# Two lists, pairs of tiles and single tiles, for both mixture-of-experts layers of a decoder kernel

## The chip, the cores and the metric

The kernel runs on one core of a Trainium2 chip. A core has five engines with queues of their own: TensorE (PE, matrix products), VectorE (DVE), ScalarE (ACT), GpSimd (POOL) and SyncE (SP, which here only issues DMAs). They meet through semaphores. The metric is the device time of one execution in microseconds (us), lower is better; where several executions were timed, their median is given.

## The reference

A decoder of two layers works on `x`, four batches of 512 tokens with 256 features (2048 tokens). Each layer is a cross-attention to a context and a feed-forward network (FFN), each behind a layer norm and with a residual sum. What matters here are the two FFNs, both with routed experts, all in float32:

```
FFN0: 8 experts, top 2 of each token, hidden width 1024
  cap = ceil(ceil(2048*2*1.25)/8) = 640 rows per expert, later rows are dropped
  h = silu(buf @ Wg.T) * (buf @ Wu.T)      W12 = [Wg; Wu], 2048 x 256 per expert
  y = h @ W3.T                             summed back with the routing weights
FFN1: 15 experts, top 3 of each token, hidden width 256, no cap
  a = gelu(g) * xh * mult ; y = a @ fc2.T  weighted sum over the 3 experts
  plus a shared expert of width 512 for every token
```

Which rows an expert gets is only known on the chip, from the router's logits. With the given inputs the kept rows per expert are 484, 320, 640, 193, 463, 226, 595, 640 in FFN0 and 678, 325, 314, 88, 187, 462, 437, 202, 452, 364, 887, 345, 474, 458, 471 in FFN1.

## The kernel before, in words

**Stages.** Attention 0 goes through the four batches; behind each batch, `route` normalises its tokens, finds the experts and ranks, and scatters the rows with indirect DMAs (the "puts", L381, on POOL) into a buffer in HBM where each expert has a region of its own (`slots` for FFN0, `xs` for FFN1). Then comes the loop over FFN0's tiles, attention 1 with the routing of FFN1, and the loop over FFN1's tiles. A tile is 128 rows of one expert, a pair is 256 neighbouring rows of one expert.

**Lists.** `listing` (L405) counts the rows of every expert and works out, in some 18 small DVE operations over all experts at once, a list of (expert, row block) entries. Two selector matmuls (L461) bring it into one row, from which SP later loads registers: `fetch0`/`fetch1` load an entry's rows with a register address, then its expert's weights. `listing` is a generator: at each `yield` it hands the turn back.

**FFN0.** After two batches a first list names three (`AHEAD`) full pairs; these are computed in the tail of attention 0 (`some_pairs`), under the routing of the last batch. In that last batch, the second list is made inside `route`, in `counted`, that is ahead of the ranks and the puts. It holds single tiles: what the three pairs have not taken. `ALWAYS0` = 24 of them always run, more of them stand in nested `If`s. For a single tile, `hidden0` puts two blocks of 128 columns into one PSUM tile (L1006, 64 matmul instructions of 128 columns), `output0` multiplies with W3 (L1024, 16 instructions of 256 columns). Every entry loads 3 MB of weights (L153) into a ring of three places; the loads stand on SP behind the entry's rows (L969).

**FFN1.** Every expert's first pair is in the program without a list, so its weights and rows have fixed addresses; the list holds further pairs, 15 of which always run. `hidden` (L1307) and the output (L1361) work with 256 rows. Weights (L1160/L1161, or L1163/L1164 with a register) have a ring of three, rows (L1332) a ring of five. The list is made after the puts of the last batch, in the tail of attention 1, where PE works through the shared expert's pieces (L1188, L1203) with their gate on DVE (L1174, L1177). Results are scattered by indirect DMAs on POOL (L1030, L1368), and read back in order at the end (L1411).

**What sets the order.** On PE, DVE, ACT and SP the order is written out: `attention` steps through time slots; in each slot it emits its own matmuls, then lets the generators that are "going" (`route`, `listing`) advance by up to two yields, with at most one piece of PE work, and then emits one piece of the other work (an AHEAD pair's piece, or a shared expert's). The first thing that PE, DVE or SP meets in its queue therefore blocks what stands behind it. The loops run as `pipeline`: in iteration p it fetches entry p+2, turns (transposes) p+1, computes the hidden part of p and the output of p-1. The last entries' `values_load` brings the length of the list into registers of all engines, for the `If`s.

## Time and profile before

Three runs took 1203.73, 1205.29 and 1206.92 us (median 1205.29).

| | |
|---|---|
| profiled execution, its own time | 1215.69 us |
| its span, first to last instruction | 1214.0 us |
| mean granted TensorE clock | 0.955 |
| PE busy | 1149.4 us (95%), 6582 instructions |
| DVE busy | 620.4 us (51%) |
| ACT busy | 459.5 us (38%) |
| POOL busy | 186.5 us (15%) |
| moved by DMA | 204.73 MB, mean 169 GB/s |
| loads of W12 and W3 | 27 each (2048 and 1024 KB) |
| loads of rows for FFN0 | 3 of 258 KB, 24 of 129 KB |
| loads of rows, w1 and fc2 for FFN1 | 30 each (258, 515 and 256 KB) |

By stages, PE busy: 270.92 us of 0 to 300 (attention 0), all of 320 to 540 (FFN0), 278.53 us of 600 to 880 (attention 1), all of 1050 to 1160 (FFN1), 27.74 us of the last 54.

A matmul in float32 shows as two instructions. Matmuls are pipelined and their ends are modelled, so a row's duration holds a tail that the next one overlaps: a pitch is read from start to start. "[1.05 <-DMA rows<-slots]" behind a line means that its engine sat idle for 1.05 us before it, until that transfer had landed.

### The profile page before, as it was taken

The page shows a single profiled execution, that of the slowest core. Times are in us where ns is not written, and L with a number is a line of the kernel's source. Part 1 is how long each engine was busy: PE and PEld are TensorE (multiplying, and loading weights), DVE is VectorE, ACT ScalarE, POOL GpSimd, SP SyncE. Part 2 cuts the span into 40 slices and gives each one's busy share as a digit, 9 for nine tenths or more (in the row PEclk, how much of TensorE's full clock was granted, in tenths as well). Part 3 has the DMA queues.
Part 4 walks back from the last instruction along what each step waited for, and adds up shares of the span by engine and source line. Part 5 has one row for each costly group of instructions (what it writes and reads, how often), then busy time and mean ns, then how long its engine had stood idle before and what let it go on. Part 6 is the DMA issues. An engine that isn't in the chain of part 4 may idle for free.

```text
span 1214.0 us, 18265 instructions
## 1 busy us (share of the span) xinstructions
PE 1149.4 (95%) x6582; PEld 738.3 (61%) x6582; DVE 620.4 (51%) x1591; ACT 459.5 (38%) x877; POOL 186.5 (15%) x274
## 2 busy tenths in 40 slices
PE   6999997999999999999999999999999999999982
PEld 3334432788999999997433333433336558888862
DVE  6677773531111111114768688867636435444426
ACT  3365464421222222223266576575653102333320
POOL 2000112042000000002000000211322402333330
PEclk7899998999999999999699999999989989999996
DMA  8999107227788888863101000001100135777737
GB/s 321 406 403 403 69 27 264 75 92 292 302 306 326 316 312 305 317 253 106 35 1 36 1 1 1 27 27 36 44 25 28 53 114 160 218 236 214 226 122 244
DMA packets 64405, 204.73 MB, mean 169 GB/s; under 512 B 9502, under 2 KB 31922, under 8 KB 57392
## 3 DMA queue, kind: packets, MB, share of 16 engines
q1 hardware_dynamic: 56144, 182.93, 42.3%
q0 software_dynamic: 8160, 20.52, 4.6%
q8 instruction: 55, 0.90, 0.3%
q14 instruction: 46, 0.38, 0.1%
HBM read 138.57 MB, written 66.70 MB: 169 GB/s over the span
## 4 chain that ended last, share of the span: by engine, by line
PE 44%; DMA 5%; DVE 4%; issue 1%; ACT 0%; POOL 0%; SPq 0%; DVEq 0%; POOLq 0%
PE sc L696 10%; PE av L735 5%; PE shared L1188 4%; PE pg L1307 3%; PE pv L1307 3%; PE pyp L1361 3%; PE sct L720 3%; DMA y<-ysb,rows 2%; DMA yr<-y 2%; PE pp L673 2%; DVE negmax L701 2%; PE shared L1203 1%; PE po L792 1%; PE pa L645 1%; PE pa L673 1%
## 5 line engine op out<-in xcount | busy, mean ns | idle before, releaser
L701 DVE TENSOR_REDUCE negmax<-sc 128x1 f32<-128x512 f32 x384 | 245.6, 683 | 67.8 <-PE sct L720 59.2
L725 ACT ACTIVATE es<-sct 128x512 f32<-128x512 f32 x384 | 208.5, 596 | 155.2 <-PE sct L720 143.6
L696 PE MATMUL sc<-kT,qT 32*128 32x512 f32 x768 | 255.5, 680 | 5.2 <-DVE negmax L701 2.8
L720 PE MATMUL sct<-qa,kT 32*128 32x512 f32 x768 | 254.3, 660 | 1.7 <-DVE qa L711 1.7
L696 PEld LDWEIGHTS sc<-kT,qT 32*128 32x128 f32 x768 | 82.6, 194 | 103.8 <-DVE negmax L701 59.8
L1015 DVE TENSOR_TENSOR hT<-pu,sg 128x256 f32<-128x256 f32 x96 | 40.8, 425 | 136.5 <-PE pu L1006 131.6
L735 PE MATMUL av<-es,v 128*32 128x512 f32 x768 | 107.2, 619 | 0.1
L1006 PE MATMUL pg<-rT,w 128*128 128x128 f32 x768 | 101.5, 275 | 0.1
L1006 PE MATMUL pu<-rT,w 128*128 128x128 f32 x768 | 101.4, 275 | 0.0
L720 PEld LDWEIGHTS sct<-qa,kT 32*128 32x128 f32 x768 | 78.9, 188 | 26.6 <-issue 16.7
L1006 PEld LDWEIGHTS pg<-rT,w 128*128 128x128 f32 x768 | 93.5, 192 | 0.4 <-issue 0.3
L1006 PEld LDWEIGHTS pu<-rT,w 128*128 128x128 f32 x768 | 93.5, 192 | 0.0
L1024 PE MATMUL py<-w,hT 128*128 128x256 f32 x384 | 86.7, 379 | 0.0
L1368 POOL DMA_INDIRECT y<-ysb,rows x60 | 59.0, 984 | 155.1 <-ACT ysb L1366 143.5
L1024 PEld LDWEIGHTS py<-w,hT 128*128 128x128 f32 x384 | 71.2, 190 | 8.7
L1011 ACT ACTIVATE sg<-pg 128x256 f32<-128x256 f32 x96 | 36.8, 383 | 101.5 <-PE pg L1006 100.5
L378 POOL COPY rows<-weight 128x2 f32<-128x2 f32 (+1 forms) x28 | 4.2, 205 | 434.5 <-DVE weight L341 258.6
L735 PEld LDWEIGHTS av<-es,v 128*32 128x32 f32 x768 | 16.0, 109 | 76.7 <-issue 70.6
L1307 PE MATMUL pg<-rTp,wp 128*128 128x256 f32 x240 | 61.8, 380 | 0.6 <-DVE rTp L1345 0.6
L1307 PE MATMUL pv<-rTp,wp 128*128 128x256 f32 x240 | 61.6, 379 | 0.0
L1030 POOL DMA_INDIRECT y<-ysb,rows x24 | 23.6, 982 | 238.7 <-ACT ysb L1028 236.3
L1174 DVE TENSOR_SCALAR aTp<-pv,wp 128x256 f32<-128x256 f32 x60 | 32.6, 544 | 51.4 <-PE pv L1307 48.3
(257 smaller groups left out, 1490.3 us busy)
## 6 DMA issues: line engine op xcount, KB each, us to landing
w<-in_W12T_dram SPq DMA_DIRECT2D x27, 2048.0 KB
xs<-empty SPq DMA_DIRECT2D x61, 516.0 KB
w<-in_W3T_dram SPq DMA_DIRECT2D x27, 1024.0 KB
wp<-in_w1p_dram SPq DMA_DIRECT2D x30, 515.0 KB
yr<-y SPq DMA_DIRECT2D x20, 512.0 KB
rows<-xs SPq DMA_DIRECT2D x30, 258.0 KB
wp<-in_fc2T_dram SPq DMA_DIRECT2D x30, 256.0 KB
slots<-empty SPq DMA_DIRECT2D x11, 516.0 KB
```

The costliest lines, as they stand in the source:

```text
L696: nc.tensor.matmul(sc, q[u][32 * j : 32 * j + 32, qt * P : (qt + 1) * P], k[u][32 * j : 32 * j + 32, :], start=True, stop=True,)
L701: nc.vector.tensor_reduce(heads[:, qt, j, HELP[s] : HELP[s] + 1], sc, AX.X, ALU.max, negate=True)
L720: nc.tensor.matmul(sc, k[u][32 * j : 32 * j + 32, kt * P : (kt + 1) * P], qa[u][32 * j : 32 * j + 32, :], start=True, stop=True,)
L725: nc.scalar.activation(t, sc, AF.Exp, scale=p["scale"])
L735: nc.tensor.matmul(av[b, g][32 * j : 32 * j + 32, :], vs[b % NV][:, kt, h : h + 32], es[u, kt, j], start=(first and kt == 0), stop=(last a ...
L1006: nc.tensor.matmul(ph[:, i * n : (i + 1) * n], w[:, c, col + i * P : col + (i + 1) * P], rT[:, c, :], start=(c == 0), stop=(c == DC - 1),)
L1011: nc.scalar.activation(sg, pg, AF.Silu)
L1015: nc.vector.tensor_tensor(h, pu, sg, ALU.mult)
L1024: nc.tensor.matmul(py, hT[f][:, i * P : (i + 1) * P], w[:, f, :], start=(f == 0), stop=(f == NF - 1))
L1188: nc.tensor.matmul(ph, w1[:, c, col : col + P], ffn1.xT[b][:, c, :], start=(c == 0), stop=(c == DC - 1),)
L1307: nc.tensor.matmul(ph[:, :n], w1[:, c, col : col + P], rhs[:, c, :], start=(c == 0), stop=(c == DC - 1),)
L1368: ins = nc.gpsimd.indirect_dma_start(out=y1, out_offset=bass.IndirectOffsetOnAxis(ap=rows[:, i, D : D + 1].bitcast(I32), axis=0), in_=ysb[ ...
```

## The change

Both FFNs get two lists: pairs of tiles, and single tiles, of which an expert has at most one.

- `listing` takes a list of kinds (`steps, width, count, out`) and runs its body once for each. For pairs, an expert's number is the count of steps 128, 384, 640, ... that its rows exceed; for singles, it is the count of steps 0, 128, 256, ... less twice the pairs. The selector's counts are first copied out of PSUM. A single list takes 5 yields, two take 11.
- FFN0: after the three AHEAD pairs, 10 pairs and 4 singles always run, instead of 24 singles. `hidden0`, `turn0`, `output0` take the width of the entry from `listed0`.
- FFN1: 24 pairs and 6 singles always run, instead of 15 fixed pairs and 15 listed ones. No entry has a fixed address any more: each takes two register loads on SP, and rows and weights of the first entries are fetched one entry after another.
- `pipeline` takes the keys of the entries, pairs first; two groups of `If`s stand behind it instead of one, and two lengths are loaded.
- Pools: the turned rows and hidden tiles of FFN0 are twice as wide; the places of the weight ring go by the order of loads.

```diff
-ALWAYS0, THEN0 = 24, (25, 26, 28, MOST0)
-ALWAYS1, THEN1 = 15, (16, 17, 19, EXTRA1)
+ALWAYS0, THEN0 = (10, 4), ((11, 12, 14, E0 * (TILES0 // 2)), (5, 6, E0))
+ALWAYS1, THEN1 = (24, 6), ((25, 26, 28, (T * K1 + E1 * (P - 1)) // PAIR), (7, 8, 10, 12, E1))
...
-    def listing(f, b, pool, bank, pairs, count, steps, out, taken=None, take=0, size=1):
+    def listing(f, b, pools, bank, tiles, kinds, take=0):
...
+        counts = pools[0].tile([P, n], F32, name="list_counts", tag="list_counts")
+        nc.vector.tensor_copy(counts, number)
+        former = None
+        for pool, (steps, width, count, out) in zip(pools, kinds):
...
+            yield V
+            more = tile("more", n, steps.shape[1])
...
+            extra = tile("extra", n)
+            nc.vector.tensor_reduce(extra, more, AX.X, ALU.add)
+            front = None
+            if former is not None:
+                front = tile("front", n)
+                nc.vector.tensor_scalar(front, former, 2.0, None, ALU.mult)
+                nc.vector.tensor_tensor(extra, extra, front, ALU.subtract)
+            elif take:
+                former = tile("former", n)
+                nc.vector.tensor_copy(former, extra)
+                less, front = tile("less", n), tile("front", n)
...
+            else:
+                former = extra
+            yield V
...
+            yield V
...
+            yield V
+            nc.vector.tensor_tensor(one, named[:, :n], one, ALU.mult)
...
+            yield PEP
+            flat = bank([1, 2 * count])
+            for i in range(2):
+                nc.tensor.matmul(
+                    flat[:, i * count : (i + 1) * count], both[:, i : i + 1], ident[:, :count], start=True, stop=True
+                )
+            nc.vector.tensor_copy(out[:, : 2 * count], flat)
...
+            run(always, last=True)
+            for i, (_, more) in enumerate(then):
+                with ExitStack() as open_:
+                    for least, keys in more:
+                        open_.enter_context(tc.If(needed[i] > least))
+                        run(keys)
+
+    def keys_of(always, then, first):
+        keys = [first, first + then[0][-1]]
+        more = [
+            [(lo, list(range(k + lo, k + hi))) for lo, hi in zip((n, *t), t)] for k, n, t in zip(keys, always, then)
+        ]
+        return [k + i for k, n in zip(keys, always) for i in range(n)], more
...
+    def listed0(j):
+        if j < AHEAD:
+            return ahead0, j, AHEAD, 2
+        j -= AHEAD
+        if j < MOST0[0]:
+            return list0[0], j, MOST0[0], 2
+        return list0[1], j - MOST0[0], MOST0[1], 1
...
     def hidden0(j, new):
-        m = 1 if j < AHEAD else 2
+        m = 2 // listed0(j)[3]
         n = PAIR // m
...
             if b == B - 1:
-                yield from listing(
-                    ffn0, b, ml1, bank, TILES0, MOST0, ffn0.some, list0, ffn0.taken, AHEAD
-                )
+                kinds = list(zip(ffn0.steps, (2, 1), MOST0, list0))
+                yield from listing(ffn0, b, ml1, bank, TILES0, kinds, AHEAD)
...
             if b == B - 1:
-                yield from listing(ffn1, b, Slices(tiles1[0]()), bank, PAIRS1, EXTRA1, ffn1.some, list1)
+                yield from listing(
+                    ffn1, b, [Slices(tiles1[0]), Slices(tiles1[0])], bank, TILES1,
+                    list(zip(ffn1.steps, (2, 1), MOST1, list1)),
+                )
...
     def fetch1(p):
         if p in rows1s:
             return
         rows1s[p] = mp.tile([P, 2, ROW], F32, name="rows1", tag="rows1", bufs=5)
-        if p == 0:
-            for j in range(3):
-                w1s[j] = weights(mp, j, "wp", 3)
-        i = p - E1
-        if i < 0:
-            src = pairs1[p * PAIRS1]
-        else:
-            r = nc.sync.value_load(list1[0:1, EXTRA1 + i : EXTRA1 + i + 1], min_val=0, max_val=E1 * PAIRS1)
-            src = pairs1[bass.ds(r, 1)].rearrange("o p s d -> p (o s) d")
-        after(nc.sync.dma_start(rows1s[p], src).ins, ffn1.puts, "rows in their places")
-        e = p if i < 0 else nc.sync.value_load(list1[0:1, i : i + 1], min_val=0, max_val=E1 - 1)
-        if p not in w1s:
-            w1s[p] = weights(mp, e, "wp", 3)
+        at, i, n, m = listed1(p)
+        r = nc.sync.value_load(at[0:1, n + i : n + i + 1], min_val=0, max_val=E1 * TILES1)
+        src = tiles_1[bass.ds(r, m)].rearrange("s p d -> p s d")
+        after(nc.sync.dma_start(rows1s[p][:, :m], src).ins, ffn1.puts, "rows in their places")
+        w1s[p] = weights(mp, nc.sync.value_load(at[0:1, i : i + 1], min_val=0, max_val=E1 - 1), "wp", 3)
...
     def output1(p):
         aT, (_, w2, _), rows = aT1s.pop(p), w1s.pop(p), rows1s.pop(p)
+        m = listed1(p)[3]
...
-        for i in range(2):
+        for i in range(m):
```

`listed1` is `listed0` for FFN1, without the AHEAD branch.

## The prediction

> **What bounds the kernel now.** I read the page first (TensorE busy 1149.4 of 1214.0 us), then the table by stretches for the two FFN stages, then the timelines at their starts and ends, because an average over stages says nothing of one stage. In the stretch rows the columns are: stretch, its length, then busy us (and instructions) of PE, weight loads, DVE, ACT and POOL, granted clock, DMA share, GB/s.

> ```profile
> 320.00:540.00 220.00, 220.00 (x1665) 210.53 (x1664) 42.19 (x100) 50.11 (x122) 20.36 (x21) 1.00 0.83 313
> 1050.00:1160.00 110.00, 110.00 (x550) 96.80 (x550) 51.33 (x99) 35.01 (x79) 37.37 (x38) 1.00 0.77 226
> ```

> In FFN0 (first row) and FFN1 (second row) PE is busy without a gap, at full clock, while DMA has 17% and 23% left. So a stage gets shorter by PE time removed, not by bytes removed. The pitches, from the PE timeline:

> ```profile
> 262.38 14.06 PE L1006 MATMUL ahead<-ahead,w 128*128 128x256 f32 x64
> 276.27 13.98 PE L1024 MATMUL ahead<-w,ahead 128*128 128x256 f32 x64
> ...
> 321.91 0.38 PE L988 MATMUL prt<-ident,rows 128*128 128x128 f32 x2
> ...
> 332.74 0.38 PE L988 MATMUL prt<-ident,rows 128*128 128x128 f32 x2
> ```

> A single tile of FFN0 takes 332.74 − 321.91 = 10.83 us; a pair of FFN1 5.62 us (1148.16 to 1153.78 in the last fence, one load per pair). A pair of FFN0 exists already, under attention 0: 276.27 − 262.38 = 13.89 us for its hidden part and, for two outputs, 290.08 (the next PE line) − 276.27 = 2 × 6.90 us.

> **FFN0 loop, ten pairs.** Routing the reference's inputs gives 484, 320, 640, 193, 463, 226, 595 and 640 kept rows, 30 tiles: three pairs done ahead, then 24 singles before, ten pairs and four singles after (the constants, so no conditional part runs). A pair costs 13.89 + 6.90 + 4 transposes at 0.11 (the next instruction starts 0.43 us after four such) = 21.2 us against 2 × 10.83 = 21.65. The matmul streams 256 columns instead of twice 128, the same array time; only the weight-load-bound 0.111 us per 128 columns becomes 0.108. Gain 10 × 0.43 = **−4.3 us**. Ten expert loads of 3 MB vanish, worth nothing, since PE covers them; without that cover 30 MB at 313 GB/s would be 96 us. The four singles keep the pitch of before.

> **FFN0 start, the longer listing.** In `route` of batch 3 the listing stands ahead of the ranks and the puts. Two lists instead of one take six more yields, and the puts release the first row fetch; on SP the first expert's load waits behind that fetch:

> ```profile
> 279.09 0.97 POOL L381 DMA_INDIRECT slots<-rows,put  x1 [0.30 <-issue]
> ...
> 281.81 0.33 SPq L969 DMA_DIRECT2D rows<-slots  x1
> 283.10 0.33 SPq L153 DMA_DIRECT2D w<-in_W12T_dram  x1
> ...
> 291.52 0.44 PE L988 MATMUL prt<-ident,rows 128*128 128x128 f32 x2 [1.05 <-DMA rows<-slots]
> ```

> Today PE comes free at 290.1 and the first hidden matmul runs at 292.1: just in time, so any delay of the puts is paid. In the built order of the changed program the last pair's eight hidden pieces (1.73 us each) start at about 261.7. The second list's selector matmul stands after the second piece on PE, at 265.2, and its 17 DVE operations at some 0.2 us, behind two gate operations, end at about 267.1: PE idles 1.9 us. Put 1 then follows piece 7, and puts 2 and 3 both piece 8 (end 278.1). POOL works off 2 × 1.27 us per put, so the last scatter ends near 285.4 instead of 280.06: 5.3 us late. Two row tiles of 258 instead of 129 KB ahead add 258 KB at 421 GB/s, 0.6 us. **+5.9 us** (3.9 if the list hides and only the queue of puts stays; 6.4 with a slower DVE). Behind it stand rows, W12 and W3 of the first pairs on SP, all late together. The 1.0 us row wait that the second single had at 300 falls under a 13.9 us hidden part: **−1.0**.

> PE now idles about 6 us there. A like gap at the end of the trace:

> ```profile
> 1185.00:1190.00 5.00, 2.21 (x5) 1.85 (x6) 5.00 (x7) 0.00 (x0) 0.00 (x0) 0.50 0.62 196
> ...
> 1187.79 7.88 PE L1203 MATMUL p<-ctxT,aTs 128*128 128x256 f32 x28 [6.31 <-DVE aTs L1177]
> ```

> After 6.31 us idle the clock is 0.50 and 28 matmuls take 7.88 instead of 28 × 0.216 = 6.05 us. **+1.7** (0 to 2). The second `If` costs PE another look at a branch; the one today costs 0.64 us (FFN0) and 1.62 us (FFN1, hidden under the reads at the end): **+1.0** (0 to 2). The two register loads three entries before the end show no PE gap today: 0.

> **Attention 1's tail, the FFN1 lists.** PE carries the shared expert there, without slack:

> ```profile
> 967.88 0.26 PE L461 MATMUL bank<-ident,shared 128*1 128x23 f32 x4
> 967.99 0.81 DVE L1174 TENSOR_SCALAR shared<-shared,ctxT 128x512 f32<-128x512 f32 x1 [0.33 <-PE shared L1188]
> ```

> Today the list's last operations precede the gate (L1174) on DVE, and the selector matmul L461 finds its operand. In the changed order the gate's two operations (0.81 + 0.69 us) stand before the last five list operations (0.7 us), so L461's successor waits from 967.96 to about 970.3: 2.3 us. The second list does the same once more: seven operations (2.0 us), two gates, ten operations (1.85 us), end near 977.4 against PE's 975.7: 1.75 us. **+4.1** (1 to 5.5). [...] The trace shows granted 0.73 in 960 to 965 after 1.29 us idle behind matmuls of 16 rows. [...]

> **FFN1 loop.** Before 30 pairs (60 tiles); 54 tiles are needed (678, 325, 314, 88, 187, 462, 437, 202, 452, 364, 887, 345, 474, 458, 471 rows): after 24 pairs, six singles. A single is 16 × 0.111 + 4 × 0.216 + 2 × 0.108 = 2.86 us on PE, so 6 × (5.62 − 2.86) = **−16.5**. But its expert load stays, and SP becomes the limit:

> ```profile
> 1148.16 0.33 SPq L1164 DMA_DIRECT2D wp<-in_fc2T_dram  x1
> 1149.47 0.38 SPq L1332 DMA_DIRECT2D rows<-xs  x1
> 1150.92 0.68 SPq L1163 DMA_DIRECT2D wp<-in_w1p_dram  x1
> 1153.78 0.33 SPq L1164 DMA_DIRECT2D wp<-in_fc2T_dram  x1
> 1155.83 0.38 SPq L1332 DMA_DIRECT2D rows<-xs  x1
> ```

> L1164 waits for the end of an iteration's output; the rows of the entry three on are issued 1.31 us later (register load between) and are turned at the next iteration's end. So an iteration lasts at least 1.31 us plus the rows' landing. The rows issued at 1155.83 were used at 1158.99: landing ≤ 3.2 us for 258 KB; crowded ones took 4.3 (1025.14 to 1029.42). [...] I take the row less 129 KB at this stage's 226 GB/s: 2.7. The iterations with the first four singles would need 3.73, 2.86, 2.86, 2.86 us and get 4.0, 4.0, 4.0 and 5.5 (one list load before the end costs 2.05 − 1.31 = 0.74 us today, two 1.5): **+5.2**. [...] At the start the three weight loads no longer go out together but 3.2 us apart; they have from about 987 to 1001, so 0.

> **End.** Four scatters stand on POOL at the end today; the last is issued at 1174.82, 3 us after PE's last output, and the reads of y1 wait for it (1179.06). Two single tiles leave two: **−2.0** (−3 to 0). All else of the end is those reads.

> **Sum**: −4.3 + 5.9 − 1.0 + 1.7 + 1.0 + 4.1 + 0.5 − 16.5 + 5.2 − 2.0 = −5.4 us. Made in the profiled execution (1215.69 us, span 1214.0 and 1.7 around it), 0.9% above the median 1205.29; the terms are short, so the difference carries over: 1199.9, say **1200.0 us** (−0.44%).

> **Rivals.**
> (a) The lists hide and rows land early: list stalls 1 instead of 4.1, puts 1.9 us earlier, row stalls 0.3 instead of 5.2: −15.3, 1190. For it: DVE is half idle. Against: the built order puts gates between list operations. 12%.
> (b) Slower: the rows of the singles land late. At 4.6 us (1042.13 to 1046.75) iterations last 5.9 us, the stalls are 2.2 + 3.0 + 3.0 + 4.5 = 12.7 us, and the sum is +2.1; at 5.2 us, +4.5, 1209.8. It decides from about 4.0 us on. For it: each single still brings 771 KB of weights. Against: crowded landings come only in the first eight pairs. 17%.
> (c) No change that can be told: list prices at their upper ends (+1.4, +0.5, +1.2) give −2.3, 1203. 20%.
> (d) The loads bind FFN0: a gain of tens of us; PE's 220.00 of 220 excludes nearly all of it. 1%.
> The forecast itself, 1196 to 1203: 50%.

> **Numbers.** 0.3% (3.6 us) is what a measurement of this kernel can tell. Faster, below 1201.7: 0.43 of the 0.50, (a) and (d): 0.56. Same: the other 0.07, 0.17 of (c), and the mild part of (b), 0.04: 0.28. Slower: the rest, 0.16. Range: 1191.5 leaves out the lower part of (a), 1208.5 the upper of (b).

> **What would show it.** FFN0's first hidden matmul 6 us after AHEAD's last output, at a clock below 1; then pairs at 21.2 us. Selector matmuls waiting for DVE about 2 us three times. Last six FFN1 entries at about 4 us with waits for rows. Wrong if the first FFN0 pair starts without a gap, if singles run at 2.9 us, or if PE no longer fills the pairs.

## The result, and the profile after

The changed kernel takes 1212.1 us (median, 1208.0 to 1216.2), the kernel before on the same chip 1206.0 us (1203.6 to 1212.4): a ratio of 1.0044, 95% interval 1.0029 to 1.0058. It is slower by 5.3 us (3.5 to 7.0), where the forecast was 1200.0 us and faster. In what follows every timed run is given as its ratio to the kernel before on its own chip; 0.1% is 1.2 us.

The two profiled executions hide this. Before's took 1215.69 us, about 10 us above its median, after's 1213.86 us, about 2 above: read naively, the traces say that the change gained 1.8 us. So stages are compared here, each against as many traces as hold the same code.

First the two loops, by stretches. The columns are as in the forecast's first fence: stretch, its length, busy us (and instructions) of PE, weight loads, DVE, ACT and POOL, granted clock, DMA share, GB/s.

```profile
320.00:540.00 220.00, 220.00 (x1131) 196.19 (x1130) 40.72 (x94) 46.37 (x114) 20.62 (x21) 1.00 0.49 181
1050.00:1140.00 90.00, 90.00 (x450) 79.25 (x449) 42.07 (x81) 28.62 (x64) 31.56 (x33) 1.00 0.80 230
```

PE is still busy without a gap in both loops, at full clock. FFN0 moves 181 instead of 313 GB/s, and nothing came of that, as PE covered the loads. The loops did what was forecast. The loss lies at their ends. This is PE's timeline of the changed kernel (start, length, engine, line, tiles, and in brackets the idle time ahead and what ended it):

```profile
266.59 0.36 PE L478 MATMUL bank<-ident,list_both 128*1 128x8 f32 x4 [1.09 <-DVE list_both L471]
...
277.79 13.98 PE L1062 MATMUL ahead<-w,ahead 128*128 128x256 f32 x64
291.61 0.60 PE L1026 MATMUL prt<-ident,rows 128*128 128x128 f32 x4
299.67 1.12 PE L1026 MATMUL prt<-ident,rows 128*128 128x128 f32 x4 [7.46 <-DMA rows<-slots]
300.58 1.91 PE L1044 MATMUL pg<-rT,w 128*128 128x256 f32 x4
...
549.57 7.07 PE L1062 MATMUL py<-w,hT 128*128 128x256 f32 x32
561.34 6.60 PE L703 MATMUL pa<-ctxT,Wk 128*128 128x512 f32 x8 [4.70 <-PEq L512]
...
975.02 0.48 PE L478 MATMUL bank<-ident,shared 128*1 128x31 f32 x4 [1.99 <-DVE shared L470]
982.32 0.37 PE L478 MATMUL bank<-ident,shared 128*1 128x15 f32 x4 [1.48 <-DVE shared L471]
...
1152.59 0.41 PE L1382 MATMUL ptp<-ident,rows 128*128 128x128 f32 x2 [1.95 <-DMA rows<-xs]
1157.70 0.63 PE L1382 MATMUL ptp<-ident,rows 128*128 128x128 f32 x2 [2.05 <-DMA rows<-xs]
...
1173.73 9.33 PE L1225 MATMUL p<-xT,ctxT 128*128 128x512 f32 x16 [4.96 <-PEq L512]
```

Two things stand out that the trace of before did not have. FFN0's first hidden matmul (L1044) is at 300.58 instead of 292.08, after 7.46 us without rows. And behind the last matmul of each FFN, PE stands for 4.70 and 4.96 us, released by its own sequencer at L512, the line of `tc.If`; the eight K matmuls behind the first of these gaps take 6.44 us from the first to the next group, those of before 3.54 (the granted clock of the changed kernel is 0.50 from 560.5 to 567.0 us). The same two places before:

```profile
545.48 7.07 PE L1024 MATMUL py<-w,hT 128*128 128x256 f32 x32
553.18 3.70 PE L673 MATMUL pa<-ctxT,Wk 128*128 128x512 f32 x8 [0.64 <-ACTq L495]
...
1173.51 7.11 PE L1188 MATMUL p<-xT,ctxT 128*128 128x512 f32 x16 [1.62 <-ACTq L495]
```

The queues at FFN0's start, POOL's puts and then SP's issues:

```profile
274.17 0.97 POOL L380 DMA_INDIRECT slots<-rows,put  x1 [3.37 <-issue]
...
283.98 0.97 POOL L380 DMA_INDIRECT slots<-rows,put  x1 [0.31 <-issue]
```

```profile
286.82 0.38 SPq L1007 DMA_DIRECT2D rows<-slots  x1
288.00 0.33 SPq L152 DMA_DIRECT2D w<-in_W12T_dram  x1
289.25 0.38 SPq L1007 DMA_DIRECT2D rows<-slots  x1
```

The puts end at 284.95 (280.06 before). The second pair's rows, whose transposes stand ahead of the first pair's hidden part on PE, are issued at 289.25 behind a W12 load and arrive at 299.67.

### The profile page after: what moved, and what is told of

Read it like the earlier page. It is cut to its first block, busy times and chain, and to the rows that moved or that the text cites. A ratio compares the mean times of both kernels' runs of the same rounds, so it can differ in the third digit from the quotient of the medians.

```text
span 1212.2 us, 16957 instructions
## 1 busy us (share of the span) xinstructions
PE 1133.9 (94%) x5914; PEld 707.5 (58%) x5914; DVE 619.4 (51%) x1623; ACT 451.7 (37%) x861; POOL 180.8 (15%) x270
## 4 chain that ended last, share of the span: by engine, by line
PE 44%; DMA 4%; DVE 4%; issue 0%; ACT 0%; SPq 0%; DVEq 0%
PE sc L726 10%; PE av L765 5%; PE pg L1349 3%; PE shared L1225 3%; PE pv L1349 3%; PE pyp L1403 3%; PE sct L750 2%; DMA y<-ysb,rows 2%; DMA yr<-y 2%; PE pp L703 2%; DVE negmax L731 2%; PE shared L1240 1%; PE pa L703 1%; PE po L822 1%; PE pa L675 1%; PE ptp L1382 1%
## 5 line engine op out<-in xcount | busy, mean ns | idle before, releaser
L1044 PE MATMUL pg<-rT,w 128*128 128x256 f32 (+1 forms) x448 | 100.1, 352 | 0.0
L1044 PE MATMUL pu<-rT,w 128*128 128x256 f32 (+1 forms) x448 | 99.9, 352 | 0.0
L1044 PEld LDWEIGHTS pu<-rT,w 128*128 128x128 f32 x448 | 77.0, 192 | 8.5
L1044 PEld LDWEIGHTS pg<-rT,w 128*128 128x128 f32 x448 | 76.5, 193 | 8.1
L1410 POOL DMA_INDIRECT y<-ysb,rows x54 | 53.1, 984 | 148.1 <-ACT ysb L1408 137.0
L1068 POOL DMA_INDIRECT y<-ysb,rows x24 | 23.6, 982 | 241.3 <-ACT ysb L1066 236.4
L1349 PE MATMUL pg<-rTp,wp 128*128 128x256 f32 (+1 forms) x240 | 57.7, 364 | 0.6 <-DVE rTp L1386 0.6
L1349 PE MATMUL pv<-rTp,wp 128*128 128x256 f32 (+1 forms) x240 | 57.3, 362 | 0.0
L222 DVE TENSOR_SCALAR rT<-prt,affine 128x256 f32<-128x256 f32 (+1 forms) x14 | 7.1, 506 | 92.7 <-PE prt L1026 92.7
```

The costliest lines, as they stand in the source:

```text
L1044: nc.tensor.matmul(ph[:, i * n : (i + 1) * n], w[:, c, col + i * P : col + (i + 1) * P], rT[:, c, :], start=(c == 0), stop=(c == DC - 1),)
L1349: nc.tensor.matmul(ph[:, :n], w1[:, c, col : col + P], rhs[:, c, :], start=(c == 0), stop=(c == DC - 1),)
L1410: ins = nc.gpsimd.indirect_dma_start(out=y1, out_offset=bass.IndirectOffsetOnAxis(ap=rows[:, i, D : D + 1].bitcast(I32), axis=0), in_=ysb[ ...
```

## The experiments

The stages below come from the traces, by the same marks in each: the end of AHEAD's last output, FFN0's first hidden matmul, the end of FFN0's last output, attention 1's first K matmul and the instruction behind its eight, an output matmul of the shared expert in attention 1's tail (the first of L1240 after 905 us), FFN1's first hidden matmul, the end of FFN1's last output, and the first read of y1. The times are us.

| kernel | to first hidden | FFN0 loop | gap to K | eight K | tail to FFN1 | FFN1 loop | to y1 reads | ratio (95%) |
|---|---|---|---|---|---|---|---|---|
| before | 1.83 | 260.47 | 0.63 | 3.54 | 80.23 | 169.34 | 7.16 | 1 |
| before_again | 1.86 | 260.60 | 0.64 | 3.54 | 77.29 | 169.85 | 7.17 | |
| before_no_if | 2.76 | 260.82 | 0.57 | 3.54 | 77.27 | 170.02 | 5.32 | 0.9977 (0.9959 to 0.9995) |
| after | 8.81 | 256.06 | 4.70 | 6.44 | 79.97 | 158.44 | 9.11 | 1.0044 (1.0029 to 1.0058) |
| no_if | 8.47 | 256.26 | 0.57 | 3.54 | 79.94 | 159.06 | 3.73 | 0.9929 (0.9910 to 0.9949) |
| pairs_if | 7.69 | 256.32 | 0.61 | 3.54 | 79.96 | 155.58 | 5.37 | 0.9960 (0.9948 to 0.9973) |
| singles_if | 9.00 | 255.51 | 0.61 | 3.54 | 81.61 | 156.77 | 5.36 | 0.9945 (0.9924 to 0.9966) |
| one_if | 8.56 | 255.96 | 2.81 | 5.23 | 79.95 | 157.19 | 5.47 | 0.9979 (0.9964 to 0.9994) |
| w12_first | 3.66 | 254.23 | 4.80 | 5.94 | 81.59 | 156.38 | 9.22 | 0.9984 (0.9968 to 0.9999) |
| puts_first | 2.87 | 254.23 | 4.94 | 4.89 | 83.25 | 156.40 | 8.25 | 0.9943 (0.9923 to 0.9962) |
| rows_ahead | 8.23 | 256.03 | 4.78 | 6.38 | 79.96 | 153.78 | 9.49 | 1.0020 (1.0006 to 1.0034) |
| ffn0_only | 8.46 | 255.93 | 4.90 | 6.28 | 77.27 | 167.97 | 7.02 | 1.0088 (1.0063 to 1.0113) |
| ffn1_only | 2.25 | 260.09 | 0.63 | 3.53 | 83.26 | 157.37 | 8.31 | 0.9922 (0.9900 to 0.9945) |

### The second branch

`no_if` leaves out both conditional parts of both FFNs.

```diff
             run(always, last=True)
-            for i, (_, more) in enumerate(then):
-                with ExitStack() as open_:
-                    for least, keys in more:
-                        open_.enter_context(tc.If(needed[i] > least))
-                        run(keys)
```

> The changed kernel with the conditional parts of both FFNs left out (with these inputs no list is longer than its fixed part, so nothing that would run is missing). Theory A, the second conditional part stands bare: TensorE's second compare-and-branch takes about 4 us (556.8 to 561.1, and 1169.0 to 1173.6) because nothing is queued behind which it could hide, and the clock is cold after it. Taking all of them away gives back the 4.1 us gap and 2.9 us of cold clock before attention 1's first K matmul, and 3.7 us by which the reads of y1 are late at the end: about 10.7 us, to about 1201.5 (0.4% under the kernel before). Rival B, the gap only stands in for another wait (the reads of y0, SP's or POOL's queue): at most 2 us come back, about 1210.

Measured: 0.9929, which is 1.15% or 13.9 us under the changed kernel. Its trace has no gap at FFN0's end (0.57 us), no cold clock there (3.54), and reads y1 3.73 us behind FFN1's last output instead of 9.11. Those are 4.1 + 2.9 + 5.4 = 12.4 us of the 13.9. Theory A holds, a little more came back than it forecast, and rival B falls: nothing took the place of the gap.

`one_if` puts one condition around both parts. Four more DVE operations per pair of lists make its cell: the excess of each count over its fixed part, their sum, and its copy.

```diff
+            with tc.If(needed[-1] > 0):
-            for i, (_, more) in enumerate(then):
-                with ExitStack() as open_:
+                for i, (_, more) in enumerate(then):
+                    with ExitStack() as open_:
...
             nc.vector.tensor_copy(out[:, 2 * count :], end[:1, n - 1 : n])
+            if over is not None:
...
+                nc.vector.tensor_scalar(passed, end[:, n - 1 : n], -float(always[2 - width]), 0.0, ALU.add, ALU.max)
...
+                    nc.vector.tensor_tensor(passed, passed, pairs_over, ALU.add)
+                    nc.vector.tensor_copy(over, passed[:1, :])
```

> The changed kernel with one outer condition around both conditional parts of each FFN: three DVE operations more per list pair put the excess of both counts over the fixed parts into one cell, so that one branch skips everything. Theory A (the price is that of a second branch, one branch hides behind the last outputs): 9 to 11 us come back, 1201 to 1203. Rival C (the price grows with the number of blocks or the length of code that is jumped over, not with the number of branches taken): nothing comes back, 1211 to 1213.

Measured: 0.9979, 7.8 us under the changed kernel. Rival C, by which nothing comes back, falls, but it is less than the 9 to 11 us of theory A: a gap of 2.81 us and eight K matmuls in 5.23 us stay at FFN0's end. So two branches are dearer than one, but this one is dearer than the single one of before. `pairs_if` and `singles_if` keep one of the two conditional parts each, in both FFNs, to see whether the code that is jumped over sets the price.

```diff
-            for i, (_, more) in enumerate(then):
+            for i, (_, more) in enumerate(then[:1]):
```

```diff
-            for i, (_, more) in enumerate(then):
+            for i, (_, more) in list(enumerate(then))[1:]:
```

> The changed kernel with the conditional parts for the single tiles left out, those for the pairs kept: one branch per FFN, and it jumps over 14 pairs (FFN0). With these inputs nothing that would run is missing. Theory A (a first branch hides behind the queued outputs, a second stands bare): as the kernel before has it, a gap of 0.6 us ahead of attention 1's first K matmul and no cold clock there, so 10 us less than the changed kernel, a ratio of 0.996. Rival L (a branch pays by where it lands or by the code it jumps over; the single outer branch kept 2.8 us and a clock near a half): a gap of 2.5 to 4 us, 6 to 8 us less than the changed kernel, 0.998 to 0.999.

> The changed kernel with the conditional parts for the pairs left out, those for the single tiles kept (the same remark): again one branch per FFN, over four single tiles in FFN0. Theory A: the same as with the pairs' branch alone, a gap of 0.6 us and a ratio of 0.996. Rival L (length of the jump): a shorter jump is cheaper than the pairs' one, 0.994 to 0.995, with a gap under 0.6 us in FFN0.

Measured: 0.9960 and 0.9945, 10.1 and 12.0 us under the changed kernel. The first K matmul of pairs_if, and then of singles_if and of one_if:

```profile
558.52 3.70 PE L703 MATMUL pa<-ctxT,Wk 128*128 128x512 f32 x8 [0.61 <-ACTq L512]
```

```profile
553.89 3.70 PE L703 MATMUL pa<-ctxT,Wk 128*128 128x512 f32 x8 [0.61 <-ACTq L512]
```

```profile
560.18 5.40 PE L713 MATMUL pa<-ctxT,Wk 128*128 128x512 f32 x8 [2.80 <-ACTq L520]
```

Either branch alone leaves a gap of 0.61 us and full clock. They jump over the parts for 14 pairs and for four single tiles, and leave the same gap, so the length of the jump does not set the price between these two: rival L falls, theory A has its numbers (0.996 forecast, 0.9960 measured; the other's interval, up to 0.9966, holds it too). What one TensorE branch takes stands in the records of its queue. First the kernel before in the stretch 545 to 566 us, then the changed kernel in 545 to 565, then pairs_if over the whole span (count, then ns as least, median and most, and first and last start):

```profile
L495 PEldq COMPARE_BRANCH  x1: 3538/3538/3538, 548.6 to 548.6; - x1
```

```profile
L512 PEldq COMPARE_BRANCH  x2: 3594/3893/4192, 552.6 to 556.8; - x2
L512 PEldq EVENT_SEMAPHORE  x2: 51/51/51, 556.7 to 561.1; - x2
```

```profile
L512 PEldq COMPARE_BRANCH  x2: 3337/3610/3883, 553.9 to 1159.4; - x2
```

In the changed kernel the first branch of FFN0 begins at 552.6, 4.0 us before the last output matmul ends (549.57 + 7.07 = 556.64), and is over before it (552.6 + 3.59 = 556.2). The first conditional part then ends with a semaphore instruction at 556.7, behind that matmul; the second branch begins at 556.8, when PE has nothing left, and ends at 561.0. So a branch is not cheap on TensorE: the records shown here take 3.34 to 4.19 us, and where one was hidden, matmuls that were queued ahead of it hid it. At FFN1's end, where the outputs of the last two single tiles have 8 matmul instructions together, even one branch is only partly hidden: in pairs_if PE waits 3.29 us there.

TensorE is not alone in this. In the changed kernel ScalarE's second branch is over at 557.3, and its next instruction comes at 560.1, where one branch alone leaves it 0.5 us (pairs_if). The K matmul waits for that instruction too: in pairs_if and one_if it is what ends the gap. The changed kernel, then pairs_if:

```profile
L512 ACTq COMPARE_BRANCH  x2: 45/48/50, 556.7 to 557.3; - x2
L512 ACTq EVENT_SEMAPHORE  x2: 17/17/17, 557.2 to 560.1; - x2
```

```profile
L512 ACTq COMPARE_BRANCH  x1: 50/50/50, 558.0 to 558.0; - x1
L512 ACTq EVENT_SEMAPHORE  x1: 17/17/17, 558.5 to 558.5; - x1
```

So with TensorE's second branch at no cost, the K matmul would have come at about 560.1 instead of 561.3 (an estimate from these lines, after one_if, where it came at 560.18). That the second part costs 4.1 us here is shown by leaving either out; most of it stands on both engines at once.

`before_no_if` is the control: the kernel before, without its conditional parts.

```diff
             run(begin, always)
-            with ExitStack() as open_:
-                lo = always
-                for hi in then:
-                    open_.enter_context(tc.If(needed > lo))
-                    run(lo, hi)
-                    lo = hi
```

> The kernel before with its two conditional parts left out (with these inputs they do not run). Theory A (a single branch hides behind the outputs that are queued ahead of it): the gap of 0.64 us goes and the reads of y1 come up to 1.5 us earlier, 0.5 to 2 us less. Rival K (each branch taken has a price of its own, since leaving all out gained 13.9 us of the changed kernel where 10.7 were expected, and one outer branch kept a gap of 2.8 us): 3 to 4 us less.

Measured: 0.9977, 2.8 us less (0.6 to 5.0). The trace shows 1.85 us of it in the reads of y1 (5.32 instead of 7.17 us behind the last output) and 0.07 us in the gap; the interval takes in both theories.

### The late start of FFN0

`w12_first` issues W12 of the first two listed pairs ahead of the rows.

```diff
         def fetch(j):
+            if j == AHEAD:
+                for i in (j, j + 1):
+                    name0(i)
+                    fetch_w12(i)
+                fetch0(j)
+            elif j == AHEAD + 1:
+                fetch0(j)
+            else:
...
```

> The changed kernel with the W12 loads of FFN0's first two listed pairs issued on SP ahead of the rows of the first. Theory D (the first hidden matmul of FFN0, 300.58 instead of 292.08, waits for the second pair's rows, which were issued at 289.25 right behind a 2 MB load and landed 10.4 us later): the rows then land about 3 to 4 us after their issue, the first hidden matmul comes at 291.5 to 294, the cold clock after it goes: 7 to 9 us less, about 1204. Rival E (the puts' delay alone is the cause and the rows land late whatever stands ahead of them): first hidden matmul at 299 or later, at most 1.5 us less, 1211.

Measured: 0.9984, 7.2 us under the changed kernel; theory D holds. PE's timeline of this kernel:

```profile
274.19 13.98 PE L1062 MATMUL ahead<-w,ahead 128*128 128x256 f32 x64
289.57 0.63 PE L1026 MATMUL prt<-ident,rows 128*128 128x128 f32 x4 [1.40 <-DMA rows<-slots]
291.28 0.66 PE L1026 MATMUL prt<-ident,rows 128*128 128x128 f32 x4 [1.08 <-DMA rows<-slots]
291.82 1.10 PE L1044 MATMUL pg<-rT,w 128*128 128x256 f32 x4
```

The puts are as late as ever (their last scatter is issued 7.8 us before AHEAD's end here and in the changed kernel, 11.2 in before_again), but two waits of 1.40 and 1.08 us are all that is left of 7.46. The stage shrinks by 5.15 us, and the loop by the 1.83 us of cold clock that followed (granted 0.56 from 300 to 305 us in the changed kernel).

`puts_first` instead makes the two lists behind the ranks and puts.

```diff
             if b == 1:
...
-            if b == B - 1:
-                kinds = list(zip(ffn0.steps, (2, 1), MOST0, list0))
-                yield from listing(ffn0, b, ml1, bank, TILES0, kinds, AHEAD)
         yield from route(ffn0, b, mr0, bank, counted)
+        if b == B - 1:
+            kinds = list(zip(ffn0.steps, (2, 1), MOST0, list0))
+            yield from listing(ffn0, b, ml1, bank, TILES0, kinds, AHEAD)
```

> The changed kernel with FFN0's two lists made behind the puts of batch 3 instead of ahead of the ranks. It splits the 8.5 us by which FFN0's first hidden matmul is late into the puts' delay and the landing of the rows behind W12. Theory O (both count: the puts end 4.9 us late, and the second pair's rows land 3.1 us later after their issue): the first hidden matmul comes 4 to 5 us earlier, no stall of 1.1 us at the list's first selector matmul, 4 to 6 us less than the changed kernel, a ratio of 1.000. Rival P (only the place of W12 counts): within 1.5 us of the changed kernel.

Measured: 0.9943, 12.2 us under the changed kernel (interval some 3 us either way), twice what was expected. Its timeline:

```profile
279.14 0.25 PE L478 MATMUL bank<-ident,list_both 128*1 128x16 f32 x4
...
292.29 0.66 PE L1026 MATMUL prt<-ident,rows 128*128 128x128 f32 x4 [1.25 <-DMA rows<-slots]
292.83 1.10 PE L1044 MATMUL pg<-rT,w 128*128 128x256 f32 x4
```

The list's selector matmul finds its operand, and the rows are issued at 280.63. Those of the second pair still take 9.2 us (issued at 283.07); they are only under way earlier. The trace accounts for 5.9 us of the start, 1.1 us of the stall at L478 and 1.8 us of clock, 8.8 in all; the rest of the 12.2 is within the two intervals and is not explained. Rival P (only W12's place counts) falls, and so does a simple sum of two causes: either edit, the earlier puts or the loads out of the rows' way, recovers nearly the whole idle time, since both bring the same rows forward against the same end of AHEAD.

### The lists of FFN1, and the two halves of the change

`ffn0_only` and `ffn1_only` join one half of each kernel; each half has its own listing and pipeline.

```diff
-                yield from listing(
-                    ffn1, b, [Slices(tiles1[0]), Slices(tiles1[0])], bank, TILES1,
-                    list(zip(ffn1.steps, (2, 1), MOST1, list1)),
-                )
+                yield from listing_old(ffn1, b, Slices(tiles1[0]()), bank, PAIRS1, EXTRA1, ffn1.some, list1)
...
-    pipeline(
-        always, [(how_many(*p), m) for p, m in zip(zip(list1, MOST1), more)],
+    pipeline_old(
+        0, E1 + ALWAYS1, [E1 + h for h in THEN1],
```

The lines show ffn0_only against the changed kernel; ffn1_only is the reverse.

> FFN0 as in the changed kernel, FFN1 as in the kernel before. Theory H, from the stages of the two traces (FFN0's first hidden matmul 8.5 us later, the loop 4.4 us shorter, the second branch's gap 4.1 and the cold clock after it 2.9 us longer): 11 us over the kernel before, about 1217 to 1219, and FFN0's half is the whole loss. Rival I, the terms of the prediction for this half (-4.3 + 5.9 - 1.0 + 1.7 + 1.0): 3.3 us over it.

> FFN1 as in the changed kernel, FFN0 as in the kernel before. Theory H (loop 10.9 us shorter, end 1.3 us longer, lists in attention 1's tail 3 to 4.6 us): 5 to 7 us under the kernel before, a ratio of 0.994 to 0.996. Rival J (the list stalls cost nothing net, as the two traces put side by side have it, -0.3 us): 9 to 10 us under it, 0.992.

Measured: 1.0088 and 0.9922. FFN0's half costs 10.6 us where theory H had 11 and the prediction's own terms 3.3; FFN1's half gains 9.4 us, as rival J had it, though its interval (6.6 to 12.1) takes in the upper end of H as well. Together they give +1.2 us, the whole change +5.3; the intervals overlap.

`before_again` is the kernel before once more, for the tail of attention 1.

> The kernel before once more, for a second trace. In the first trace attention 1 and the shared expert (from the first K matmul to FFN1's first hidden matmul) took 449.4 us, though the same code took 443.3 us in the kernel without conditional parts. Theory Q (the first trace holds some longer stretches of half clock, chance and not the kernel): about 443 us here, so that the lists of FFN1 cost the changed kernel about 3 us (446 in seven traces). Rival R (449 is what this kernel takes): 447 to 450, and the lists gain something.

From the first K matmul to FFN1's first hidden matmul it took 446.0 us, between the two expectations. The part that holds the lists is clearer (the column "tail to FFN1"): 77.29, 77.27 and 77.27 us in the three other traces with before's lists, 80.23 in the first. With the changed kernel's lists twelve traces have 79.9 to 83.3 us, on average 81.3, in three groups about 1.65 us apart (left out are singles_first, whose first entry is a single, and puts_first_one_if, on a chip where the kernel before took 1219 us). The clock records tell the groups apart: 6.83, 10.24 and 13.65 us of the stretch run at a granted clock of 0.50, in pieces of 3.41 us, while PE's waits add up to 5.7 to 5.9 us in all of them. With before's lists the waits are 2.36 us, with 10.24 us at half clock (3.65 and 13.65 us in the first trace, which is how it hid the price). So the lists cost 2.7 to 6.0 us, on average 4.0; with equal time at half clock (10.24 us) they cost 4.3, of which 3.5 are waits.

`list_at_once` takes ffn1_only and drops the four yields within each list of FFN1.

```diff
-            yield V
```

> FFN0 of the kernel before, FFN1 of the changed one, and in FFN1's listing the four yields between groups of DVE operations of each list taken out, so that the scheduler puts each list's operations on DVE in one piece. Theory M (TensorE idles 1.99 and 1.48 us at the selector matmuls because gate operations stand between the list's on DVE): these waits shrink to under 0.5 us each, 2 to 3 us less than with the yields, a ratio of 0.990. Rival N (the same DVE time then delays the shared expert's gates, for which TensorE waits instead): within 1 us of the 0.9922 of before.

Measured: 0.9959 (0.9941 to 0.9977). The waits at the two selector matmuls are 1.33 and 1.98 us instead of 1.99 and 1.48: theory M falls, the same DVE work is waited for in other portions, and the kernel is not faster than ffn1_only. By its middle value it is 4.5 us slower, where rival N allowed 1; the two intervals overlap, and this difference is not explained.

### The single tiles of FFN1

`rows_ahead` fetches each entry's rows one entry earlier.

```diff
     def fetch1(p):
+        fetch_rows1(p)
+        if p < MOST1[0] - 0 and p + 1 < ALWAYS1[0]:
+            fetch_rows1(p + 1)
...
+    def fetch_rows1(p):
         if p in rows1s:
             return
-        rows1s[p] = mp.tile([P, 2, ROW], F32, name="rows1", tag="rows1", bufs=5)
+        rows1s[p] = mp.tile([P, 2, ROW], F32, name="rows1", tag="rows1", bufs=6)
```

> The changed kernel with the rows of each entry of FFN1 fetched one entry earlier (rows buffers 6 instead of 5), in the pairs and in the singles. Theory F (the last six entries wait for rows that SP issues only behind the fc2 load of the entry before): the waits of 0.67, 1.95 and 2.05 us and the cold clock after them (1.6 us) go, and the entries shorten to near 2.9 us: 5 to 7 us less, about 1206. Rival G (the 771 KB of expert weights per single are the limit): the waits move to the hidden and output matmuls, at most 2 us less, 1210 to 1211.

Measured: 1.0020, 2.9 us under the changed kernel, about midway between the two. No single waits for rows any more, the loop is 153.78 instead of 158.44 us, but two entries wait for weights:

```profile
1150.41 0.68 PE L1349 MATMUL pg<-rTp,wp 128*128 128x128 f32 x4 [1.53 <-DMA wp<-in_w1p_dram]
1153.74 0.68 PE L1349 MATMUL pg<-rTp,wp 128*128 128x128 f32 x4 [0.23 <-DMA wp<-in_w1p_dram]
```

`singles_first` asks whether that is bandwidth: ffn1_only with the same edit, a fourth buffer of weights and the singles ahead of the pairs.

```diff
-            w1s[p] = weights(mp, nc.sync.value_load(at[0:1, i : i + 1], min_val=0, max_val=E1 - 1), "wp", 3)
+            w1s[p] = weights(mp, nc.sync.value_load(at[0:1, i : i + 1], min_val=0, max_val=E1 - 1), "wp", 4)
...
+    always = always[ALWAYS1[0] :] + always[: ALWAYS1[0]]
```

> FFN0 of the kernel before; FFN1 of the changed kernel with its six single tiles ahead of its 24 pairs, rows one entry ahead and four buffers of expert weights instead of three. If the singles' waits are those of loads issued one entry too late, the deeper fetching takes them away (4 to 5 us), and the pairs' 16 output matmuls at the end hide more of the first branch than a single's 8 do (1 us): a ratio of 0.987. If the singles are bound by the bandwidth of their weights, the waits move to the weights and the ratio stays at 0.992.

Measured: 0.9932 (0.9908 to 0.9956). Transposes of consecutive singles in its trace:

```profile
1002.70 0.38 PE L1481 MATMUL ptp<-ident,rows 128*128 128x128 f32 x2
...
1005.57 0.38 PE L1481 MATMUL ptp<-ident,rows 128*128 128x128 f32 x2
...
1008.44 0.38 PE L1481 MATMUL ptp<-ident,rows 128*128 128x128 f32 x2
```

Singles run at 2.87 us here, PE's own pace, without a wait. The first three had their loads under attention 1, but the others keep that pace too; a wait of 1.39 us for weights comes at the first pair. The loop is 153.67 us, 3.7 less than in ffn1_only. So with loads issued early enough the singles were bound by PE. In the time it shows no gain over ffn1_only (0.9922): the intervals are as wide as what was to be gained, and PE's gap at the end was still 5.41 us (6.46 in ffn1_only).

### Edits put together

`together` is the changed kernel with one_if, w12_first and rows_ahead; `ffn1_best` is ffn1_only with the same three; `puts_first_one_if` is the changed kernel with puts_first, one_if and rows_ahead. Their diffs are those above.

> The changed kernel with all three edits that paid alone: one outer condition per FFN, W12 ahead of the rows at FFN0's start, rows one entry ahead in FFN1. If they are independent (ratios 0.9979, 0.9984 and 1.0020 against 1.0044): 7.8 + 7.2 + 2.9 = 17.9 us less than the changed kernel, about 1194, a ratio of 0.990. If they share idle time and cold clock: 12 us less, about 0.995.

> FFN0 of the kernel before (single tiles, one branch), with W12 of its first two entries issued ahead of the rows; FFN1 of the changed kernel with one outer condition and rows one entry ahead. If the gains add: 0.9922 less 0.0024 for the rows, 0.002 to 0.003 for the condition at FFN1's end and 0.001 for FFN0's start (1.05 us of wait there): a ratio of 0.986, about 1191. If the end is bound by the reads of y1 and not by the branch: 0.989.

> The changed kernel with FFN0's lists behind the puts, one outer condition per FFN and rows one entry ahead in FFN1. If the three gains add (ratios 0.9943, 0.9979 and 1.0020 against 1.0044, so -1.01, -0.65 and -0.24%): a ratio of 0.985 to 0.986, about 1189, under both kernels and under the half change (FFN1 alone, 0.9922). If they fall short of their sum as the three gains did that were put together before (0.9924 where 0.990 was expected): 0.988 to 0.989. If the start's gain was chance (its trace accounts for 8.8 us, the timed runs for 12): 0.988.

Measured: 0.9924 (0.9900 to 0.9948), 0.9921 (0.9894 to 0.9947) and 0.9893 (0.9856 to 0.9931). The first falls short of the sum of its parts (0.990) by less than its interval; ffn1_best gained nothing over ffn1_only that can be seen. The last is the fastest by its middle value, 1.1% under the kernel before and 1.5% under the changed one, with the whole change in it. Its interval overlaps that of ffn1_only, so which of the two is better stays open. Whether gains add isn't settled: 0.985 to 0.989 were all on the list, and the interval holds most of that.

## Why the prediction was wrong, point by point

The terms of its sum, and what the stages show. The values measured are differences of the table's rows, of the traces that hold the same code.

| term | forecast | measured |
|---|---|---|
| FFN0 loop, ten pairs, and the second single's row wait | -4.3 - 1.0 | -6.2 (254.23 against 260.47) |
| cold clock at FFN0's start | +1.7 | +1.8 (256.06 against 254.23) |
| FFN0 start | +5.9 | +8.1 (8.81 against 1.83, and the stall of 1.09 at L478) |
| second branch at FFN0's end | +1.0 | +7.0 (gap 4.70 against 0.63, eight K matmuls 6.44 against 3.54) |
| FFN1's lists, with clock | +4.1 + 0.5 | +4.0 (2.7 to 6.0) |
| FFN1 loop | -16.5 + 5.2 | -12.0 (nine traces at 157.3 against four at 169.3) |
| end | -2.0 | -1.8 from fewer scatters, +3.7 from the second branch |

The right column sums to +4.6 us; measured were +5.3 (3.5 to 7.0). One reading under it was a little off: the row wait of the second single, taken as 1.0 us, is 0.75 us in the trace of before (300.22).

**The step that failed** is "The second `If` costs PE another look at a branch; the one today costs 0.64 us (FFN0) and 1.62 us (FFN1, hidden under the reads at the end): +1.0 (0 to 2)". It took what was left uncovered of the first branch for the price of a branch. The uncovered rest was small because the last outputs' 32 matmuls lay over it; the trace of before had the duration of the whole, 3.5 us from 548.6 on, in the records of TensorE's queue. A second branch directly behind has no such cover, and part of its gap stands on ScalarE as well, as shown above. It cost 7.0 us in FFN0, more than half of it the gap and the rest the cold clock behind it, and 3.7 us at the end, where the forecast saw none at all since it counted only PE: the reads of y1 came late (9.11 us behind the last output, and 5.37 with one branch), and everything after them follows. On GpSimd each conditional part that is skipped ends with a semaphore instruction, of 1.33 us here. The changed kernel in 1160 to 1182 us has two of them, pairs_if in 1150 to 1182 has one:

```profile
L512 POOLq INC_SWDGE_SEM  x2: 1329/1330/1330, 1173.8 to 1176.3; - x2
```

```profile
L512 POOLq INC_SWDGE_SEM  x1: 1329/1329/1329, 1164.0 to 1164.0; - x1
```

The first read of y1 goes out right behind the last of them, at 1177.88 and at 1165.59. The 7.0 and 3.7 us, 10.7 in all, stand in place of 1.0, and would by themselves carry the forecast from -5.4 to +4.3.

**FFN0's start** was the right mechanism and too small. The list stall was 1.09, not 1.9 us, and the puts ended 4.9, not 5.3 us late. But "Two row tiles of 258 instead of 129 KB ahead add 258 KB at 421 GB/s, 0.6 us" should have been 3.1: the second pair's rows took 10.4 us from issue to use (289.25 to 299.67), where they took 7.3 in before_again (281.17 to 288.44). Bytes by rate does not give that; with W12 out of the way 2.48 us were left of the wait of 7.46.

**FFN1's loop and lists** came out near the forecast, in part by luck. The steps between transposes at the loop's end took 5.40, 4.57, 5.02, 5.11, 4.53 and 2.87 us (the last one counted to its hidden part), the waits for rows were 0.67, 1.95 and 2.05 us (4.7 in all, 5.2 forecast); in the step of 4.53 us no wait stands but half clock, which the forecast did not have there. The issue of one single's rows came 3.41 us behind its weight load (1146.93 to 1150.34), where 1.31 were assumed, and the landing was as short as 2.25 us there; the two errors met.

**The clock behind the list gaps** differs between executions. The gap of 1.99 us costs no clock in the changed kernel's trace; in singles_if half clock begins at 962.7, 1.7 us behind the same gap (which ends at 961.01). The twelve matmuls behind that gap took 5.42 us in the changed kernel and 7.11 us in singles_if and in w12_first. The stretches with it in the changed kernel and in singles_if, granted clock in the third column from the right:

```profile
970.00:975.00 5.00, 3.03 (x8) 1.00 (x6) 3.76 (x14) 0.69 (x1) 0.00 (x0) 1.00 0.08 28
```

```profile
960.00:965.00 5.00, 3.94 (x10) 1.86 (x11) 3.34 (x14) 0.69 (x1) 0.00 (x0) 0.77 0.00 0
```

In one_if the eight K matmuls behind the gap of 2.81 us take 5.23 us, where pairs_if takes 3.54, and in the changed kernel's own trace half clock begins right behind FFN1's waits of 1.95 and 2.05 us (1157.7):

```profile
1155.00:1165.00 10.00, 7.95 (x48) 7.32 (x47) 3.94 (x12) 2.42 (x6) 1.97 (x2) 0.83 0.73 231
```

So gaps of 1.95 to 2.81 us were followed by half clock in some executions and not in others. The +0.5 us in the sum is a term that no run shows: behind the same gap the runs had nothing in the changed kernel, and 1.69 us (7.11 less 5.42) in singles_if and w12_first, near the 1.7 (0.5 + 1.2) of rival (c).

Of the rivals, none described what happened. Rival (b) has the right sign by another mechanism: the rows that were waited for landed 2.25 to 3.9 us behind their issue (1150.34 to 1152.59, 1153.79 to 1157.70), below the 4.0 from which it decides. The one that could have been worked out, a second branch without cover, stood as a term of +1.0 (0 to 2) and not among them.

## What to carry to other kernels

Price a branch by the duration of its record on each engine and by the time to the engine's next instruction, not by the idle time that it leaves today: that is only what its cover does not hide (0.64 us of 3.54 in FFN0 of the kernel before), and here the cover served one branch. Where a conditional part is added, ask what is queued ahead of it on TensorE; one condition in place of two gave back 7.8 us, where leaving one of the two out gave 10.1 and 12.0. And where a bulk load stands between two small transfers that the same consumer needs, order them by need before counting bytes (here 7.46 us of wait became 2.48).

## What the runs showed of the hardware that was not expected

What TensorE does in that time can be seen among the DMA packets. The profile lists two queues of the kind "instruction". In each of the 42 long records a packet of 16 KB starts on one of them, q8, and the branch ends 1.3 to 1.5 us after such a packet has landed (in puts_first once 2.2); in the two short records none starts. The packets of q8 (their number, MB, share of 16 engines' time) in the changed kernel during FFN0's first branch (552.6 to 556.2), then during its second (556.8 to 561.0); its short branch (1167.9 to 1168.4) has no such line:

```profile
q8 instruction: 1, 0.02, 2.1%
```

```profile
q8 instruction: 2, 0.03, 4.0%
```

So the long records go with such a packet and the short ones with none; whether the branch waits for it is not shown, as no run moved the code to test it. A wait for queued matmuls does not fit, as the branch with matmuls ahead of it (3.59 us) and the one with none (4.19 us) are both long, and both have the packet.

One outer branch left a gap of 2.81 us at FFN0's end where either inner one left 0.61. The gap was ended by ScalarE: its next instruction came 2.7 us after its branch (557.4 to 560.1) and 0.5 us in pairs_if (558.0 to 558.5). In all 15 places where ScalarE came on 2.0 us or more after a branch, a packet of 8 KB of the other instruction queue, q14, lies in between, but that queue has packets at other times as well. Why one layout of the code needs it and another does not, no run here shows.
